# Routing scales as stacked float32r parts, with a reordered head, seam and end, in an attention and gated feed-forward kernel

## The chip, the cores and the metric

The kernel runs on one core of one Trainium2 chip. The metric is the device time of one execution in microseconds (us); lower is better. A profile is one execution taken apart by engine: PE (TensorE, matrix products), DVE (VectorE), ACT (ScalarE), POOL (GpSimd) and SP (SyncE, which here issues most of the transfers).

## The reference

Four sequences of 512 tokens with 1024 channels go through one layer. All is float32.

```python
xn = layernorm(x)                        # over the 1024 channels, no scale or shift
q, k, v = xn @ Wq, xn @ Wk, xn @ Wv      # 16 heads of 64; rotary embedding on q and k
attn = softmax(causal(q @ k.T) / 8)
s = (attn @ v) @ Wo
routing = softmax(xn @ gate_w.T)         # 8 experts
in_scale = routing @ in_channel_scale    # 8 x 1024
out_scale = routing @ out_channel_scale  # 8 x 1024
f = ((xn * in_scale) @ sign(weight).T) * out_scale + bias
out = x + s * silu(f)
```

## The kernel before

Tokens are cut in tiles of 128 (four to a sequence). Activations lie transposed in SBUF, with channels on the partitions. Projections and the output product use one level of Strassen's scheme with seven products (`form_w`, `form_x` and `form_a` build the sums S and T on DVE), in float32. The order of TensorE is written out by hand (`manual_schedule(engines={PE})` at L69), and in the head that of DVE and ACT as well. Elsewhere the Tile scheduler orders the instructions of DVE, ACT, POOL and SP; a call wrapped in `keep_in_program_order` keeps its place.

There are four stages.

*The head* (L612 to L638) loads four token tiles and the first weights. `statistics` (L158) takes two bn halves, their aggregate and a standard deviation on ACT; `normalize` (L172) scales a tile; `transpose_x` (L183) turns it by PE, and ACT copies it to X. The first four matmuls of `project(0, 0)` stand between the transposes of tiles 1 and 2.

*The attention stage* loops over 16 groups (4 sequences by 4 groups of two head pairs; L682). Each step projects the group k (`project`, L263) and weaves in the pieces of group k-1's attention: scores (L370), softmax on DVE, ACT and POOL, transposes of the probabilities (`transpose_p`, L435), values (L449). In the first group of a sequence `router` (L474) computes its routing: 32 small matmuls, softmax, a transpose, and a store of the eight rows per tile to `rt_d` in DRAM. `make_sign` (L524) makes the signs of the feed-forward weight.

*The seam* (L829 to L858) holds the attention of the last group, together with the feed-forward of the first two token pairs. `dense` issues a piece of the feed-forward and `sum_wo` (L764) a piece of the Strassen sums t1 to t4 of Wo.

*The output stage* (L953) loops over eight pairs q of token tiles: `project_out` (L879) is the seven-product output projection. Between its products stand the scales of pair q+1; then follows its feed-forward `ffn` (L773).

The scales are products with only eight contraction rows, one per expert. `load_xn` (L538) places the eight rows of routing at partitions 0, 32, 64 and 96 by four SP transfers; `in_scales` (L563) then runs 16 matmuls of 128 columns over the four row groups and multiplies the activations by the result; `out_scales` (L595) runs four of 512 columns. Both are float32. `split` (L582) cuts the scaled activations into HI, rounded to float32r, and LO, the rest; the ff product with the signs is two float32r matmuls per chunk.

*The end* is the last `project_out`: product 4, product 3, eviction by DVE, stores by POOL (a whole row tile) and SP (two half tiles).

Of the kernel before, what the change touches and what calls it, by code (L numbers as in the profile page):

```python
# [51 lines left out]
def attn_gated_ffn_kernel(  # L52
# [45 lines left out]
    isc = cp.tile([P, E], F32, name="isc")  # L98
    osc = cp.tile([P, E], F32, name="osc")
# [6 lines left out]
    rt_d = dp.tile([B, TPB, NE, P], F32, name="rt_d")  # L106
# [49 lines left out]
    MV = {}  # L156

    def statistics(b, t):  # L158
        xt = xin[b, t]
        stats = st.tile([P, 2, 6], F32, tag="bn", name=f"bn_{b}_{t}")  # L160
        for j in range(2):

            tc.keep_in_program_order(
                nc.vector.bn_stats(stats[:, j, :], xt[:, j * HALF : (j + 1) * HALF])
            )
        mv = st.tile([P, 2], F32, tag="mv", name=f"mv_{b}_{t}")
        nc.vector.bn_aggr(mv, stats)
        std = st.tile([P, 1], F32, tag="std", name=f"std_{b}_{t}")
        nc.scalar.activation(std, mv[:, 1:2], AF.Sqrt, bias=eps)
        MV[b, t] = mv, std  # L170
# [8 lines left out]
    def layernorm(b, t):  # L179
        statistics(b, t)  # L180
        normalize(b, t)

    def transpose_x(b, t, g):  # L183
# [8 lines left out]
        if g == 0 and b > 0:  # L192
            nc.vector.tensor_copy(dst, tp)
        else:
            nc.scalar.copy(dst, tp)
# [67 lines left out]
    def project(b, g):  # L263

        for m in range(3):
# [56 lines left out]
            yield from product(r, SF[key, 3], TF[b, 3])  # L322
            yield from product(p, SF[key, 2], TF[b, 2])
# [7 lines left out]
            ps, p, r = halves(3)  # L331
            yield from product(r, SF[key, 1], TF[b, 1])
# [141 lines left out]
    def router(b, step):  # L474
        if step == 0:
# [10 lines left out]
            R["lg"] = st.tile([P, P], F32, tag="r", name=f"lgs_{b}", bufs=2)  # L486
            nc.scalar.copy(R["lg"], lg)
        elif step == 1:
# [5 lines left out]
            ex = st.tile([P, TPB, 32], F32, tag="r", name=f"rex_{b}", bufs=2)  # L494
            nc.gpsimd.memset(ex, 0.0)
# [11 lines left out]
            )  # L507
            R["ex"] = ex
        else:
            rt = bank(f"rt_{b}")[:, :P]  # L510
            nc.tensor.transpose(rt, R["ex"].rearrange("p t e -> p (t e)"), ident)
            rT = st.tile([P, P], F32, tag="r", name=f"rT_{b}", bufs=2)
            nc.vector.tensor_copy(rT, rt)
            for t in range(TPB):
                nc.sync.dma_start(out=rt_d[b, t], in_=rT[32 * t : 32 * t + NE, :])


    staged = {}

    def load_sign(n):  # L520
        staged[n] = xip.tile([P, E], F32, tag="x", name=f"wb_{n}")
        nc.sync.dma_start(out=staged[n], in_=wb[n // 4, n % 4])

# [14 lines left out]
    def load_xn(q):  # L538
# [10 lines left out]
        RT[q] = rtp.tile([P, 2, P], F32, tag="rt", name=f"rt_{q}")  # L549
        for j in range(4):  # L550
            nc.sync.dma_start(
                out=RT[q][32 * j : 32 * j + NE, :, :],
# [10 lines left out]
    def in_scales(q, banks=ring_banks):  # L563

        ps = [v.rearrange("p (i r q) -> p i r q", i=2, r=2) for v in banks(f"is_{q}")]
        for r in range(2):
            for i in range(2):
                for j in range(4):
                    p0, c = 32 * j, 4 * r + j
                    nc.tensor.matmul(  # L570
                        ps[j][:, i, r, :],
                        lhsT=isc[p0 : p0 + NE, c * P : (c + 1) * P],
                        rhs=RT[q][p0 : p0 + NE, i, :],
                        start=True,
                        stop=True,
                    )
        by_j = XP[q].rearrange("p i (r j) q -> p i r j q", j=4)
        for j in range(4):
            xs = by_j[:, :, :, j, :]
            nc.vector.tensor_tensor(xs, xs, ps[j], op=ALU.mult)  # L580

    def split(q):  # L582

        HI[q] = hl.tile([P, 2, NC, P], F32R, tag="hi", name=f"hi_{q}")
        LO[q] = hl.tile([P, 2, NC, P], F32R, tag="lo", name=f"lo_{q}")
        for i in range(2):
            for c in range(0, NC, 4):
                xs, hi, lo = (v[:, i, c : c + 4, :] for v in (XP[q], HI[q], LO[q]))
                nc.scalar.copy(hi, xs)
                nc.vector.tensor_tensor(lo, xs, hi.bitcast(F32), op=ALU.subtract)  # L590
# [4 lines left out]
    def out_scales(q, banks=ring_banks):  # L595
        ps = banks(f"os_{q}")
        for n in range(4):
# [3 lines left out]
                lhsT=RT[q][32 * n : 32 * n + NE, i, :],  # L601
                rhs=osc[32 * n : 32 * n + NE, k * HALF : (k + 1) * HALF],
# [9 lines left out]
    for t in range(TPB):  # L612
        load_x(0, t)
    for m in range(3):
# [3 lines left out]
    nc.sync.dma_start(out=gw[:, :, :NE], in_=gate_wT.rearrange("(c p) e -> p c e", p=P))  # L618

    first = project(0, 0)  # L620
    with tc.manual_schedule(engines={DVE, ACT}):
        statistics(0, 0)
        for t in range(TPB):
            if t + 1 < TPB:
                statistics(0, t + 1)
            if t == 2:
                next(first)
            normalize(0, t)
            for g in range(2):
                transpose_x(0, t, g)  # L630
            for _ in range((0, 3, 3, 0)[t]):
                next(first)
        for n in (3, 1, 2):
            form_w(keys[0], n)
        next(first)
        for n in (3, 1, 2, 4):
            form_x(0, n)
# [44 lines left out]
    for k, (b, g) in enumerate(groups):  # L682
# [3 lines left out]
        if k == 1:  # L686
            for t in range(TPB):
                nc.sync.dma_start(out=isc[32 * t : 32 * t + NE, :], in_=in_scale)
                nc.sync.dma_start(out=osc[32 * t : 32 * t + NE, :], in_=out_scale)
        extra = []  # L690
        if g == 0:
            extra = [lambda s=s: router(b, s) for s in range(3)]
# [12 lines left out]
        if g == 0:  # L705
            extra += [
                lambda: (load_sign(2 * b), load_sign(2 * b + 1)),
                lambda: None,
                lambda: make_sign(2 * b),
                lambda: make_sign(2 * b + 1),  # L710
            ]

        step = max(1, (len(pieces) + len(extra)) // (len(extra) + 1))
        for n, e in enumerate(extra):
            pieces.insert(min(len(pieces), (n + 1) * step + n), e)
        if b == B - 1:
# [310 lines left out]
```

## Time and profile before

| what | value |
|---|---|
| median of three runs | 1200.04 us (1199.61 to 1200.54) |
| the profiled execution's own time | 1199.76 us |
| its span | 1198.0 us |
| PE busy | 1176.7 us (98%) |
| DVE busy | 751.4 us (63%) |
| POOL busy | 515.8 us (43%) |
| ACT busy | 490.1 us (41%) |

The span runs from the first to the last event of the profile; the time of an execution is a little longer. A line of a view gives start, duration, engine, source line, operation and tiles (output first). What stands in brackets is idle time of the engine just before, and what ended it. The ends of matmuls are modelled, so the distance between starts says how long PE was held. A float32 matmul leaves two records, a float32r matmul one.

### The profile page before, as it was taken

To read this page: it belongs to the slowest core of one execution; us is meant where nothing else is said; L and a number is where in the kernel's file an instruction comes from. 1 tells how busy PE (TensorE), PEld (TensorE's weight loads), DVE (VectorE), ACT (ScalarE), POOL (GpSimd) and SP (SyncE) were. 2 spreads that over 40 slices of the span, in tenths; PEclk is the share of its full clock that TensorE was granted. 3 is DMA by queue.
4 is the path that set the end of the run, shared out by engine and by line. 5 is a ranking of instruction groups with operands and counts; after the bars stand their busy time and mean duration, and the time that the engine had idled before them with its cause. 6 is when DMAs were issued, how large, how long until landed. Compare 5 with 4: busy or idle time off the path is not lost.

```text
span 1198.0 us, 18167 instructions
## 1 busy us (share of the span) xinstructions
PE 1176.7 (98%) x6920; PEld 892.5 (74%) x6920; DVE 751.4 (63%) x1365; ACT 490.1 (41%) x1132; POOL 515.8 (43%) x565
## 2 busy tenths in 40 slices
PE   7999999999999999999999999999999999999998
PEld 5988888887888887788888878788664546655663
DVE  7767777676767767676776766656673543354342
ACT  3464545445465534546553443545431221122120
POOL 0462535245253524435353534525436334533543
PEclk9999999999999999999999999999999999999999
DMA  9423233222233313223234221210505412431320
GB/s 309 143 71 113 91 106 115 80 80 89 86 108 99 128 61 101 80 84 119 82 114 149 80 80 47 86 44 29 195 20 189 162 50 93 141 119 59 106 71 35
DMA packets 57127, 120.28 MB, mean 100 GB/s; under 512 B 4624, under 2 KB 38032, under 8 KB 50896
## 3 DMA queue, kind: packets, MB, share of 16 engines
q1 hardware_dynamic: 54880, 111.26, 28.5%
q0 software_dynamic: 2160, 7.87, 1.6%
q8 instruction: 54, 0.88, 0.3%
q14 instruction: 33, 0.27, 0.1%
HBM read 93.88 MB, written 25.23 MB: 99 GB/s over the span
## 4 chain that ended last, share of the span: by engine, by line
PE 91%; DVE 5%; ACT 2%; issue 1%; POOL 0%; DMA 0%; ACTq 0%; DVEq 0%
PE pj L284 33%; PE wo L891 16%; PE pj L292 13%; PE ff L779 9%; PE ptp L441 6%; PE pv L457 6%; PE sc L375 5%; PE xtp L189 1%; DVE nmx L390 1%; ACT p L393 1%; PE is L570 1%; PE os L599 1%; DVE sg L530 1%; ACT sw L254 1%; ACT sw L253 0%
## 5 line engine op out<-in xcount | busy, mean ns | idle before, releaser
L403 POOL TENSOR_SCALAR p<-p,rs 128x128 f32<-128x128 f32 (+3 forms) x256 | 170.5, 679 | 180.0 <-DVE rs L401 180.0
L393 ACT ACTIVATE p<-sc,nmx 128x128 f32<-128x128 f32 (+3 forms) x256 | 132.4, 523 | 159.7 <-DVE nmx L390 157.0
L284 PE MATMUL pj<-T,S 128*128 128x256 f32 x768 | 183.1, 381 | 0.1
L284 PEld LDWEIGHTS pj<-T,S 128*128 128x128 f32 x768 | 139.8, 190 | 19.2 <-issue 2.3
L339 POOL TENSOR_TENSOR part<-part,part 128x256 f32<-128x256 f32 x48 | 35.2, 734 | 227.4 <-ACT part L338 206.7
L284 PE MATMUL pj<-X,w 128*128 128x256 f32 x512 | 122.9, 381 | 0.0
L256 POOL TENSOR_TENSOR sw<-sw,sin_sb 128x512 f32<-128x512 f32 x64 | 84.1, 1314 | 86.4 <-ACT sw L254 86.4
L233 DVE TENSOR_TENSOR S<-w 128x512 f32<-128x512 f32 x96 | 81.8, 853 | 39.2 <-PE pj L284 34.0
L390 DVE TENSOR_REDUCE nmx<-sc 128x2 f32<-128x512 f32 (+3 forms) x128 | 103.6, 820 | 2.5
L779 PE MATMUL ff<-sg,hi 128*128 128x512 f32 x256 | 103.5, 404 | 0.0
L441 PE MATMUL ptp<-ident,p 128*128 128x128 f32 x640 | 95.6, 273 | 6.9 <-POOL p L403 4.8
L284 PEld LDWEIGHTS pj<-X,w 128*128 128x128 f32 x512 | 92.8, 191 | 11.5 <-issue 0.5
L779 PE MATMUL ff<-sg,lo 128*128 128x512 f32 x256 | 99.8, 390 | 0.0
L447 ACT COPY pT<-ptp 128x512 f32<-128x512 f32 x96 | 56.0, 586 | 99.5 <-PE ptp L441 99.0
L441 PEld LDWEIGHTS ptp<-ident,p 128*128 128x128 f32 x640 | 78.4, 141 | 23.0 <-POOL p L403 6.0
L292 PE MATMUL pj<-S,T 128*128 128x128 f32 x768 | 92.1, 277 | 0.0
L253 ACT ACTIVATE sw<-c 32x512 f32<-32x512 f32 x128 | 80.4, 628 | 22.9 <-DVE c L311 21.1
L292 PEld LDWEIGHTS pj<-S,T 128*128 128x128 f32 x768 | 88.1, 192 | 1.7
L257 POOL TENSOR_TENSOR rot<-rot,sw 128x512 f32<-128x512 f32 x64 | 82.7, 1292 | 4.8
L375 PE MATMUL sc<-rot,rot 64*128 64x384 f32 (+3 forms) x512 | 82.0, 449 | 0.0
L254 ACT ACTIVATE sw<-c 32x512 f32<-32x512 f32 x128 | 80.4, 628 | 1.7
L457 PE MATMUL pv<-pT,v 128*64 128x256 f32 (+3 forms) x512 | 76.0, 439 | 0.0
(123 smaller groups left out, 1961.8 us busy)
## 6 DMA issues: line engine op xcount, KB each, us to landing
w<-in_wqkv SPq DMA_DIRECT2D x48, 1024.0 KB
x<-in_x SPq DMA_DIRECT2D x16, 512.0 KB
xn_d<-X SPq DMA_DIRECT2D x16, 512.0 KB
at_d<-at SPq DMA_DIRECT2D x32, 256.0 KB
xp<-xn_d SPq DMA_DIRECT2D x16, 512.0 KB
ap<-at_d SPq DMA_DIRECT2D x16, 512.0 KB
xr<-in_x SPq DMA_DIRECT2D x16, 512.0 KB
wb<-in_wb SPq DMA_DIRECT2D x8, 512.0 KB
```

What stands on the lines that cost most here:

```text
L254: nc.scalar.activation(sw[r + 32 : r + 64, :], c[r : r + 32, :], AF.Copy, scale=sc)
L256: nc.gpsimd.tensor_tensor(sw, sw, sin_sb, op=ALU.mult)
L284: nc.tensor.matmul(ps, lhsT=wq[:, k, :], rhs=xq[:, k, :], start=(k == 0), stop=(k == 3))
L292: nc.tensor.matmul(ps[:, j * P : (j + 1) * P], lhsT=xq[:, k, j * P : (j + 1) * P], rhs=wq[:, k, :], start=(k == 0), stop=(k == 3),)
L375: nc.tensor.matmul(ps[:, h, :], lhsT=Q[u][r : r + D, i * P : (i + 1) * P], rhs=K[u][r : r + D, : (i + 1) * P], start=True, stop=True,)
L390: nc.vector.tensor_reduce(nmx, ps, AX.X, ALU.max, negate=True)
L393: nc.scalar.activation(pt[:, h, :], ps[:, h, :], AF.Exp, bias=nmx[:, h : h + 1], accum_out=ssum[:, h : h + 1],)
L403: nc.gpsimd.tensor_scalar(pt[:, h, :], pt[:, h, :], rs[:, h : h + 1], 1.0, op0=ALU.mult, op1=ALU.mult,)
L441: nc.tensor.transpose(tp[:, k, :], probs(u, i)[:, h, j * P : (j + 1) * P], ident)
L457: nc.tensor.matmul(pv[r : r + D, j * P :], lhsT=V[u][:, j, r : r + D], rhs=PT[u][:, n, o : o + (TPB - j) * P], start=(j == 0), stop=(j == ...
L779: nc.tensor.matmul(acc, lhsT=part[q][:, i, c, :], rhs=sg[4 * k + c // 2][:, (c % 2) * HALF : (c % 2 + 1) * HALF], start=(c == 0 and part i ...
L891: nc.tensor.matmul(ps, lhsT=lhs[:, k, :], rhs=rhs[:, k, :], start=(k == 0), stop=(k == 3))
```

## The change

*Scales.* Routing and channel scales are each split into a float32r part and the exact rest, and stacked in 32 rows instead of 8: the routing rows are (high, high, low, low), the scale rows alternate between high and low by blocks of eight, so that one float32r product over 32 rows sums all four combinations. `router` makes the routing parts with five more DVE operations; `load_scales` loads each scale table sixteen times over by small SP transfers, and `split_scales` makes its parts on ACT and DVE, selected by the column `is_high`. Scale matmuls become 8 of 256 columns and 4 of 512, all float32r with 32 rows. The routing loads go through POOL's queue.

*Order.* The pieces of the router have fixed places; the first sequence's group 0 holds the scale splitting, and the signs are made in groups 4, 8, 12 and 13 instead of 0, 4, 8 and 12. The very first weight runs product (S1, T1) before (S2, T2).

*Head.* 42 transposes of the identity come first, and 14 more after the first tile. bn halves are interleaved with the normalization; the first weight is loaded by halves between the tiles; the last X copy goes to DVE.

*Seam.* `split` works by token tile i, with two buffers of half the size. `sum_wo` keeps program order, and the t4 sums move here from the first `project_out`.

*End.* For the last pair, what can be combined ahead of a product is combined on POOL (`ahead_of`); product 3 is computed in two halves of 256 columns; stores go by half tiles and quarter tiles over SP and ACT.

The core of the diff:

```diff
+    high = cp.tile([P, 8], F32, name="high")
...
-        if g == 0 and b > 0:
+        if (g == 0 and b > 0) or (g == 1 and (b, t) == (0, TPB - 1)):
             nc.vector.tensor_copy(dst, tp)
...
             yield from product(r, SF[key, 3], TF[b, 3])
+            if pos == 0:
+                bank3 = halves(3)
+                yield from product(bank3[2], SF[key, 1], TF[b, 1])
             yield from product(p, SF[key, 2], TF[b, 2])
...
+            hi = st.tile([P, TPB, NE], F32R, tag="rhi", name=f"rhi_{b}", bufs=1)
+            nc.vector.tensor_copy(hi, exv)
+            hi = hi.bitcast(F32)
+            for n in (3, 2):
+                nc.vector.tensor_tensor(
+                    ex[:, :, n * NE : (n + 1) * NE], exv, hi, op=ALU.subtract
+                )
+            for n in (1, 0):
+                nc.vector.tensor_copy(ex[:, :, n * NE : (n + 1) * NE], hi)
...
+    def load_scales(src):
+        v = xip.tile([P, E], F32, tag="x", name="scales")
+        for t in range(P // NE):
+            nc.sync.dma_start(out=v[NE * t : NE * (t + 1), :], in_=src)
+        scales.append(v)
+
+    def split_scales(dst):
+        v = scales.pop(0)
+        nc.vector.tensor_reduce(is_high[:, 0:1], high, AX.X, ALU.max)
+        nc.vector.tensor_scalar(
+            is_high[:, 1:2], is_high[:, 0:1], -1.0, 1.0, op0=ALU.mult, op1=ALU.add
+        )
+        nc.scalar.copy(dst, v)
+        nc.vector.tensor_tensor(v, v, dst.bitcast(F32), op=ALU.subtract)
+        nc.vector.tensor_scalar(v, v, is_high[:, 1:2], None, op0=ALU.mult)
+        nc.vector.scalar_tensor_tensor(
+            dst, dst.bitcast(F32), is_high[:, 0:1], v, op0=ALU.mult, op1=ALU.add
+        )
...
-        RT[q] = rtp.tile([P, 2, P], F32, tag="rt", name=f"rt_{q}")
+        RT[q] = rtp.tile([P, 2, P], F32R, tag="rt", name=f"rt_{q}")
         for j in range(4):
-            nc.sync.dma_start(
-                out=RT[q][32 * j : 32 * j + NE, :, :],
+            nc.gpsimd.dma_start(
+                out=RT[q][32 * j : 32 * j + 32, :, :],
...
         for r in range(2):
-            for i in range(2):
-                for j in range(4):
-                    p0, c = 32 * j, 4 * r + j
-                    nc.tensor.matmul(
-                        ps[j][:, i, r, :],
-                        lhsT=isc[p0 : p0 + NE, c * P : (c + 1) * P],
-                        rhs=RT[q][p0 : p0 + NE, i, :],
+            for j in range(4):
+                rows, c = slice(32 * j, 32 * j + 32), 4 * r + j
+                nc.tensor.matmul(
+                    ps[j][:, r, :, :],
+                    lhsT=isc[rows, c * P : (c + 1) * P],
+                    rhs=RT[q][rows, :, :],
...
-                lhsT=RT[q][32 * n : 32 * n + NE, i, :],
-                rhs=osc[32 * n : 32 * n + NE, k * HALF : (k + 1) * HALF],
+                lhsT=RT[q][32 * n : 32 * n + 32, i, :],
+                rhs=osc[32 * n : 32 * n + 32, k * HALF : (k + 1) * HALF],
...
+    def keep_warm(n):
+        idle = bank("idle")[:, :P]
+        for _ in range(n):
+            nc.tensor.transpose(idle, ident, ident)
+
+    keep_warm(42)
...
+        half_statistics(0, 0, 0)
+        half_statistics(0, 0, 1)
+        deviation(0, 0)
         for t in range(TPB):
             if t + 1 < TPB:
-                statistics(0, t + 1)
-            if t == 2:
+                half_statistics(0, t + 1, 0)
+            else:
+                form_w(keys[0], 3)
+            normalize(0, t)
+            transpose_x(0, t, 0)
+            if t + 1 < TPB:
+                half_statistics(0, t + 1, 1)
+                deviation(0, t + 1)
+            transpose_x(0, t, 1)
+            if t == 0:
+                keep_warm(14)
+            for _ in range((0, 4, 3, 0)[t]):
                 next(first)
...
-    split(0)
     for n in range(5):
         transpose_p(w, n)
+    split(0, 0)
     scores_1(units)
+    split(0, 1)
     values(w)
...
+    split(1, 0)
     out_scales(1, score_banks)
     dense(gates, 4)
...
-    split(1)
+    split(1, 1)
     scores_02(units)
     gates = gated(1)
-    sums = iter([(2, c) for c in range(4)])
-    dense(gates, 9)
+    dense(gates, 5)
+    sums = iter([(n, c) for n in (2, 4) for c in range(4)])
+    dense(gates, 5)
...
+        def ahead_of(i, k, u):
+            cols = slice(k * HALF, (k + 1) * HALF)
+            c = work.tile([P, HALF], F32, tag="g", name=f"uz_{i}_{k}")
+            nc.gpsimd.tensor_tensor(c, u, Z[q, i][:, cols], op=ALU.mult)
+            nc.gpsimd.tensor_tensor(c, c, XR[i][:, cols], op=ALU.add)
+            return c
+
+        def finish_last(i, cols, ps, c, queue):
+            z = Z[q, i][:, cols]
+            nc.vector.tensor_tensor(z, ps, z, op=ALU.mult)
+            nc.vector.tensor_tensor(z, z, c, op=ALU.add)
+            queue.dma_start(out=out[rows[i], cols], in_=z)
...
+        c01 = ahead_of(0, 1, u2)
+        nc.sync.dma_start(out=out[rows[1], HALF:], in_=Z[q, 1][:, HALF:])
+        finish_last(1, slice(0, HALF), ps, c10, nc.scalar)
+        for n in range(2):
+            ps = ps_wo.tile([P, TH], F32, tag="wo", name=f"wo_{q}_3_{n}")
+            part_n = slice(n * TH, (n + 1) * TH)
+            for k in range(4):
+                nc.tensor.matmul(
+                    ps,
+                    lhsT=SA[q, 4][:, k, :],
+                    rhs=b22[:, k, part_n],
+                    start=(k == 0),
+                    stop=(k == 3),
+                )
+            finish_last(
+                0, slice(HALF + n * TH, HALF + (n + 1) * TH), ps, c01[:, part_n], (nc.scalar, nc.sync)[n]
+            )
```

## The prediction

> **What bounds the kernel now.** I read the page first: engine shares, then the chain that ended last.
>
> ```profile
> PE 1176.7 (98%) x6920; PEld 892.5 (74%) x6920; DVE 751.4 (63%) x1365; ACT 490.1 (41%) x1132; POOL 515.8 (43%) x565
> PE 91%; DVE 5%; ACT 2%; issue 1%; POOL 0%; DMA 0%; ACTq 0%; DVEq 0%
> ```
>
> TensorE is the bound nearly everywhere. A change can win only by giving PE less to do, or where PE stands idle. The table of stages says where it stands idle.
>
> ```profile
> core 0: us, PE busy (x) PEld busy (x) DVE busy (x) ACT busy (x) POOL busy (x), PEclk, DMA share, GB/s
> 0.00:25.00 25.00, 16.07 (x133) 13.59 (x134) 17.67 (x32) 8.78 (x17) 1.50 (x11) 1.00 0.94 327
> 25.00:838.00 813.00, 808.97 (x5399) 675.04 (x5398) 566.38 (x1077) 402.68 (x959) 356.24 (x414) 1.00 0.28 92
> 838.00:897.40 59.40, 56.51 (x321) 40.05 (x320) 44.16 (x77) 25.10 (x64) 24.60 (x28) 1.00 0.29 104
> 897.40:1168.00 270.60, 270.60 (x1016) 153.05 (x1015) 114.87 (x170) 51.72 (x91) 122.27 (x104) 1.00 0.34 111
> 1168.00:1198.00 30.00, 24.55 (x59) 10.72 (x57) 8.30 (x12) 1.80 (x3) 11.20 (x9) 0.99 0.09 35
> ```
>
> Third column less second: 8.9 us idle in the head, 4.0 in all of the attention stage, 2.9 in the seam, none in the output stage, 5.5 at the end. The PE timeline of one scale step shows the work that the change touches.
>
> ```profile
> 925.74 2.74 PE L891 MATMUL wo<-wo,ap 128*128 128x512 f32 x6
> 928.41 1.17 PE L570 MATMUL is<-rt,isc 8*128 8x128 f32 x32
> 929.52 3.70 PE L891 MATMUL wo<-xp,S 128*128 128x512 f32 x8
> 936.58 1.14 PE L599 MATMUL os<-osc,rt 8*128 8x512 f32 x8
> 937.65 0.70 PE L891 MATMUL wo<-xp,S 128*128 128x512 f32 x1
> ```
>
> Ends are modelled, so I use starts: in_scales holds PE from 928.41 to 929.52 (1.11 us), out_scales from 936.58 to 937.65 (1.07). A float32 matmul leaves two records: 16 matmuls are 32 records.
>
> **What the Trainium skill says.** (1) "FP8 and Floating Point Precision", TensorE Precision Notes: true FP32 takes four passes through the array, reduced-precision FP32 reads the value truncated. The trace agrees: a float32 product of 512 columns takes 2 records at 429 ns, 858 ns; a float32r ff matmul of 512 columns starts every 227 ns (3.8 times less). (2) "TensorE: Matmul & The Clock Gate", Part 3 (packing small matmuls): K=32 matmuls in different row groups run side by side, 4 of N=512 measured 3.07 times faster. Here 8 out_scales records take 1.07 us, 134 ns each against 429 alone, 3.2 times. (3) The same page, Parts 1 and 4: the clock doubles after some 3.4 us of activity, and transposes are said not to count. The head shows
>
> ```profile
> 8.37 1.94 PE L189 MATMUL xtp<-ident,x 128*128 128x128 f32 x8 [8.37 <-DVE x L177]
> 10.59 1.97 PE L189 MATMUL xtp<-ident,x 128*128 128x128 f32 x8 [0.28 <-DVE x L177]
> 14.39 1.04 PE L189 MATMUL xtp<-ident,x 128*128 128x128 f32 x8
> ```
>
> Eight transposes take 1.9 us cold, 1.0 warm; warm came by 14.39, when only 2 us of ordinary matmuls had run. So transposes seem to count, against the page; not proved. (4) "DMA: Bandwidth & Descriptors", SWDGE vs HWDGE: a float32r destination counts as a cast, possible only from GpSimd. That explains why the routing loads move from SP to POOL; before.py has no such load.
>
> **The change, part by part.**
>
> *Scales.* in_scales: 8 float32r matmuls of 256 columns instead of 16 float32 of 128; out_scales: 4 float32r of 512 instead of 4 float32. All four row groups stay in use. Column passes fall to a quarter in both. If all shrinks with them: 1.1/4 = 0.28 us each. If instead a fixed part stays: four groups at the ideal share of 227 ns stream 0.23 us, 0.90 in four passes, so about 0.2 of the 1.1 is fixed, and 0.43 remains. I take 0.40. Eight pairs of token tiles: 8 x (1.11 + 1.07 - 0.80) = **11.0 us**, all on the path, as PE has no idle time around them. Ends: 0 (no side by side) to 12.9; a loss is the rival below.
> Beside it: each router gains five DVE operations of about 0.2 us and loses a memset; split_scales has two 128x1024 sets, some 3.5 us each by the T rows (1.2 to 1.3 us); they stand in group 0, where DVE also loses sign making. DVE is 70% busy in that stage and appears in no PE wait there. 32 small scale loads of about 0.3 us (the isc rows on SP) hold SP for 10 us from about 17 us, but the next weight load has to wait until about 27 us anyway. POOL gets 4 routing loads per pair; an output store occupies it 0.57 to 0.64 us, so 2.5 us per pair against 18 of 41 us busy: covered. They stand ahead of POOL's u2 addition, which has product 4 and 3 (6.9 us) to be late in. SP loses those loads. All these: 0, bounds -1 to +2.
>
> *Head.* The instruction order puts 42 dummy transposes first. Start about 1.5 us (identity ready), 4 us cold at 0.24 (16), 26 warm at 0.11: done at about 8.3. The first normalized tile comes at 7.8 instead of 8.2 (one bn half instead of two ahead of it, less two tiny is_high operations). From there I step through: X copy g0 at 9.0 to 9.5, std_1 behind it in ACT's order at 9.8 (**new: std of t+1 queues behind X copy of t**), normalize 1 ends 10.8, normalize 2 at 13.4, its transposes behind 4 matmuls at 13.9, std_3 at 15.4, S3 in the gap, normalize 3 ends 16.4, last copy (now DVE) 18.2, T3 19.4, T2 and S2 23.6. The T, S products of the first key end at about 27.1; before, at 27.58 with one router transpose of 0.1 among them. Faster transposes are mostly eaten by the new ACT order. Gain **0.4 us**; ends +1.5 (warm early) and -3 (never warm: 42 x 0.24 = 10 us).
>
> *Seam.* Waits of PE in 876 to 900:
>
> ```profile
> PE ptp L441 <- DVE z_t L789: 1.1, 1, 1.1
> PE ptp L441 <- POOL p L403: 0.8, 2, 0.6
> ```
>
> The first is DVE doing t4 sums (1.0 to 1.6 us) ahead of the ff evictions; the second is scores_02 evicted behind 3.6 us of split. Pinned sums put t4 later, and splitting by tile moves half of it ahead. A further 0.8 us at 838 to 846 stems from an lo piece ahead of a pT copy; only part of it leaves, as one wait hangs on a POOL addition that stays. What is late next: POOL p, by about 1 us less. I take **1.8** of 2.8; ends 0.5 and 2.8. The sums now run beside the values; t4 is needed only by product 4.
>
> *End.*
>
> ```profile
> 1192.59 0.70 DVE z_t L940
> ...
> 1193.39 0.69 DVE z_t L941
> ```
>
> Then SP stores 256 KB at 1194.11, beside 512 KB from POOL at 1193.3; DMA is busy until about 1196.7. After: two 256-column halves cost PE nothing (8 records at 216 ns, 1.73 us, twice: 3.46 against 3.43). The last DVE pair is 2 x 0.42 instead of 2 x 0.69: 0.5 us. Row 1 and the first half are stored earlier, from SP and ACT queues, so only 128 KB is left: at 400 GB/s (the DMA row there) 0.3 us instead of 1.9. POOL's c01 must be ready by 1191.3 (chain: p5 at 1186.4, three operations of 1.27: 1190.2). Gain **1.6**; ends 0.5 and 2.2.
>
> *Sum.* 11.0 + 0.4 + 1.8 + 1.6 = 14.8. The profiled execution took 1199.76 us (span 1198.0 and 1.76 around it), 0.28 below the median of 1200.04. 1199.76 - 14.8 = **1185.0 us**.
>
> **Rivals.**
> - *Packing without gain (0.10).* The float32r groups run one after the other: 8 x 114 or 4 x 227 ns is 0.91 us plus 0.2, so 1.1 each as now; scales give 0. For: only full-array float32r is in the trace. Against: float32 packs 3.2 times. 1199.76 - 3.8 = **1196.0**.
> - *Head lost (0.10).* The warm transposes stay cold and end at 11.7, 3.3 us after their tile; the 14 more fall into DVE's wait. 1185.0 + 0.4 + 3 = **1188.4**. For: the page's remark. Against: the head rows above.
> - *Slower (0.03).* On PE in the scale steps, stacked float32r groups run singly and in four passes: in_scales 8 x 0.43, out_scales 4 x 0.86, with 0.4 fixed 7.3 us a pair instead of 2.18, +41 in eight, less 3.8: **1237**. It decides from a pair above 2.65 us. Against: the 227 ns rows are single passes.
> - *Nothing of it moves (0.02)*: scale steps stay, and a late POOL or DVE in the attention stage returns 4 us: **1200**.
>
> **How the numbers follow.** The main case has 0.75; its own range is 1181.5 to 1189 by the ends above (scales 0.28 each, warm early, seam whole: -3.5; POOL p, head and end short: +4). The range 1181.5 to 1192 takes in the head rival and half-packed scales, leaving out packing without gain and the slow cases. About 0.2% (2.4 us) is what a measurement here can tell from no change. Faster by more: 0.95; within: 0.02; slower: 0.03.
>
> **What would show it.** in_scales and out_scales start to next start at 0.3 to 0.5 us each (above 1.0: packing failed); PE's 25 to 838 stage shorter by the scale steps in it, its waits on POOL p still about 4 us; xtp at 1.0 us from the first; first T product at about 19.7; PE waits of 876 to 900 below 1 us; span ending some 3.5 us after the last matmul instead of 5.4. A long first-tile wait behind the dummies, or new PE waits on DVE or POOL after 838, would make me wrong.

## The result, and the profile after

| | before | after |
|---|---|---|
| median of four runs each | 1200.17 us (1199.61 to 1200.54) | 1192.38 us (1191.28 to 1192.48) |
| ratio, 95% interval | | 0.9933 (0.9916 to 0.9951) |
| the profiled execution, its span | 1199.76, 1198.0 us | 1192.43, 1190.7 us |

The changed kernel is 7.8 us faster by the medians; 14.8 had been forecast. Line numbers below are those of the changed kernel unless an experiment or the kernel before is named. First the page's engine shares, its row of granted PE clock, and its share of the chain:

```profile
PE 1174.0 (99%) x6760; PEld 895.1 (75%) x6760; DVE 760.6 (64%) x1397; ACT 492.3 (41%) x1133; POOL 536.5 (45%) x597
PEclk9989999999999999999999999999999999999999
PE 94%; DVE 3%; ACT 1%; DMA 1%; issue 0%; POOL 0%; SPq 0%; ACTq 0%; DVEq 0%
```

PE is busy for less time and nearly all of the span, as meant. But there is an 8 in the clock row, in the third slice, some 60 to 90 us after the start. The table of stages says where PE is idle:

```profile
core 0: us, PE busy (x) PEld busy (x) DVE busy (x) ACT busy (x) POOL busy (x), PEclk, DMA share, GB/s
0.00:25.00 25.00, 21.93 (x188) 19.31 (x189) 16.78 (x31) 6.77 (x15) 1.80 (x13) 1.00 0.93 324
25.00:830.00 805.00, 797.86 (x5246) 664.62 (x5245) 566.43 (x1093) 400.71 (x942) 355.46 (x414) 1.00 0.29 94
830.00:900.00 70.00, 67.96 (x421) 51.28 (x420) 51.82 (x91) 28.68 (x81) 35.35 (x43) 1.00 0.29 100
900.00:1160.00 260.00, 260.00 (x837) 146.27 (x836) 116.34 (x171) 53.72 (x93) 129.76 (x118) 1.00 0.36 117
```

Second column less third: the attention stage, 4.0 us idle before, now has 7.1. The waits of PE name it:

```profile
PE pj L304 <- DVE S L253: 6.1, 1, 6.1
PE ptp L468 <- DVE pT L472: 1.6, 1, 1.6
...
PE ptp L468 <- POOL p L430: 1.0, 2, 0.5
```

A single wait of 6.1 us is new. The waits on POOL p, 4.0 us before, fell to 1.0. The PE timeline of the scale step shows the part that came as forecast:

```profile
929.91 0.51 PE L624 MATMUL is<-rt,isc 32*128 32x256 f32 x8
930.35 3.70 PE L994 MATMUL wo<-xp,S 128*128 128x512 f32 x8
...
937.42 0.50 PE L652 MATMUL os<-osc,rt 32*128 32x512 f32 x4
937.85 3.70 PE L994 MATMUL wo<-xp,S 128*128 128x512 f32 x8
```

From start to next start: in_scales 0.44 us (1.11 before), out_scales 0.43 (1.07). Over eight pairs that is 8 x (2.18 - 0.87) = 10.5 us.

Now the stall. The PE timeline of group 1 before, and the same stretch after:

```profile
55.17 3.72 PE L284 MATMUL pj<-X,w 128*128 128x256 f32 x16
58.73 2.75 PE L284 MATMUL pj<-T,S 128*128 128x256 f32 x12
61.41 1.99 PE L375 MATMUL sc<-rot,rot 64*128 64x512 f32 x8
```

```profile
55.48 3.72 PE L304 MATMUL pj<-X,w 128*128 128x256 f32 x16
65.34 5.04 PE L304 MATMUL pj<-T,S 128*128 128x256 f32 x12 [6.14 <-DVE S L253]
70.31 1.99 PE L402 MATMUL sc<-rot,rot 64*128 64x512 f32 x8
```

The ACT and DVE timeline after, of the same time:

```profile
60.08 1.04 ACT L572 CAST osc<-scales 128x1024 fp32r<-128x1024 f32 x1
61.15 1.33 DVE L573 TENSOR_TENSOR scales<-scales,osc 128x1024 f32<-128x1024 f32 x1 [0.77 <-ACT osc L572]
62.52 0.75 DVE L574 TENSOR_SCALAR scales<-scales,is_high 128x1024 f32<-128x1024 f32 x1
63.31 1.28 DVE L575 SCALAR_TENSOR_TENSOR osc<-osc,is_high,scales 128x1024 fp32r<-128x1024 f32 x1
64.51 1.29 DVE L253 TENSOR_TENSOR S<-w 128x512 f32<-128x512 f32 x2
```

Read from the bottom: PE waits for S3, one of the sums that `form_w` builds, of group 1's first weight. S3 takes 0.69 us and needs nothing new: PE had used the raw weight without a wait at 55.48. But in DVE's in-order queue it stands behind the three operations that split the out scales (61.15 to 64.51, 3.4 us; the texts on record say 3.3), and these wait for their cast on ACT, which stands behind the first softmax's exponentials in ACT's queue. After the gap the 12 records hold PE from 65.34 to 70.31, 0.41 us each against 0.22 for the same records of before (58.73 to 61.41): another 2.3 us lost to the clock, which the view grants at 0.55 there. From start to start the gap itself costs 6.3 us (55.48 to 65.34, before 55.17 to 58.73), so 8.6 us together; the texts on record below split the same sum as 6.1 and 2.5.

### The profile page after: what moved, and what is told of

Its sections match the earlier page's. It is cut to its first block, busy times and chain, and to the rows that moved or that the text cites. A ratio compares the mean times of both kernels' runs of the same rounds, so it can differ in the third digit from the quotient of the medians.

```text
span 1190.7 us, 17943 instructions
## 1 busy us (share of the span) xinstructions
PE 1174.0 (99%) x6760; PEld 895.1 (75%) x6760; DVE 760.6 (64%) x1397; ACT 492.3 (41%) x1133; POOL 536.5 (45%) x597
## 4 chain that ended last, share of the span: by engine, by line
PE 94%; DVE 3%; ACT 1%; DMA 1%; issue 0%; POOL 0%; SPq 0%; ACTq 0%; DVEq 0%
PE pj L304 33%; PE wo L994 16%; PE pj L312 16%; PE ff L874 9%; PE sc L402 6%; PE pv L484 6%; PE ptp L468 6%; PE xtp L209 1%; DVE nmx L417 1%; ACT p L420 1%; PE lg L506 1%; DMA x<-in_x 1%; DVE sc L413 0%; PE os L652 0%; PE is L624 0%
## 5 line engine op out<-in xcount | busy, mean ns | idle before, releaser
L430 POOL TENSOR_SCALAR p<-p,rs 128x128 f32<-128x128 f32 (+3 forms) x256 | 167.9, 669 | 182.5 <-DVE rs L428 182.5
L276 POOL TENSOR_TENSOR sw<-sw,sin_sb 128x512 f32<-128x512 f32 x64 | 85.6, 1337 | 90.2 <-ACT sw L274 90.2
L253 DVE TENSOR_TENSOR S<-w 128x512 f32<-128x512 f32 x96 | 78.4, 818 | 30.8 <-PE pj L304 27.0
L277 POOL TENSOR_TENSOR rot<-rot,sw 128x512 f32<-128x512 f32 x64 | 83.0, 1297 | 4.9
```

The lines of the kernel that those rows point to most:

```text
L276: nc.gpsimd.tensor_tensor(sw, sw, sin_sb, op=ALU.mult)
L277: nc.gpsimd.tensor_tensor(rot, rot, sw, op=ALU.add)
L430: nc.gpsimd.tensor_scalar(pt[:, h, :], pt[:, h, :], rs[:, h : h + 1], 1.0, op0=ALU.mult, op1=ALU.mult,)
```

## The experiments

Two theories of the stall stood against each other at first: the *place* of the split operations in DVE's queue, and the *32 small loads* of the scale tables, which held SP's queue (0.29 us each, all but one of them between 20.6 and 33.6 us) and so delayed the next weight. Two rows cut each run into comparable parts, whatever moved ahead of them: the start of the products (X, S) of the first key (27.58 us before, 27.78 after) ends the head, and "the v row", the transposes that wait for DVE v at the seam's beginning (840.52 and 844.18), ends the attention stage.

### e1: one transfer per scale table

```diff
-        for t in range(P // NE):
-            nc.sync.dma_start(out=v[NE * t : NE * (t + 1), :], in_=src)
+        nc.sync.dma_start(out=v, in_=src[None, :, :].to_broadcast((P // NE, NE, E)))
```

> The changed kernel, but each scale table is loaded by one SP transfer that repeats its eight rows, in place of sixteen. Theory A: the 6.1 us stall of PE at 59 us comes from DVE's order in group 1 (S3 of group 1's first weight, L253, stands behind the osc split), and that order was made because the 32 small loads hold SP's queue ahead of that weight's load. With one load the weight goes out at about 28 us instead of 33.7, S3 stands ahead of the first softmax, the stall is gone and the time is 1192.4 - 6.1 = 1186.3. Rival B: PE at that place is short of something else (the new splitting work on DVE and ACT itself is too much for group 0): the stall stays above 3 us and the time above 1189.

1190.71 us (ratio to before 0.9921, 0.9906 to 0.9936). The wait on S went, and another came in the router:

```profile
41.88 0.45 PE L547 MATMUL rt<-ident,rex 128*128 128x128 f32 x1 [4.65 <-DVE is_high L567]
```

With the tables there early, three of the splits' operations came between the small operations of the router's softmax on DVE (30.4 to 41.7 us). The clock fell again: 0.89 over 30 to 60 us. So the loads only decided *where* in DVE's queue the splits fell; taking them away moved the stall.

A second cost rides on this one. The router's last small operations, pushed back, ran beside the rotary products on POOL (L276 and L277, from 35.25 us on). The DVE timeline of e1, then that of the changed kernel, where these operations were done by 33.5, before POOL's products began at 34.08:

```profile
36.00 1.29 DVE L531 TENSOR_TENSOR rex<-rex,rrs 128x32 f32<-128x32 f32 x1
37.55 1.07 DVE L536 CAST rhi<-rex 128x32 fp32r<-128x32 f32 x1
```

```profile
32.46 0.19 DVE L531 TENSOR_TENSOR rex<-rex,rrs 128x32 f32<-128x32 f32 x1
32.69 0.18 DVE L536 CAST rhi<-rex 128x32 fp32r<-128x32 f32 x1
```

L531 to L543 took 4.8 us in e1 and 1.0 us in the changed kernel. How much of the 4.65 us is this and how much the splits themselves was not tried apart.

### e2: the three DVE operations of the out split left out

```diff
         nc.scalar.copy(dst, v)
+        if dst is osc:
+            return
         nc.vector.tensor_tensor(v, v, dst.bitcast(F32), op=ALU.subtract)
```

The low parts of the out scales are missing from its result.

> The changed kernel with its 32 loads; the three DVE operations of the osc split (L573 to L575) are left out, so that the low parts of the out scales are missing. Theory A: S3 of group 1 then starts right after the last softmax reciprocal, at about 60.5 instead of 64.5, and PE waits about 2 us instead of 6.1; time about 1188.3. Rival (the late weight load itself holds S3): S3 stays at 64 us or later, PE still waits about 6 us, time about 1192.

1185.55 us in the one run, PEclk full in every slice. All 32 loads were kept, and this is what stayed of the wait (PE timeline):

```profile
60.66 2.83 PE L304 MATMUL pj<-T,S 128*128 128x256 f32 x12 [1.92 <-DVE S L253]
```

4.2 us less wait and 6.9 us less time: most of the difference is the clock, which a gap of 1.9 us left at full speed (12 records in 2.76 us instead of 4.97). The three operations ahead of S3 were the cause of 4.2 us of the wait; the other 1.9 us stayed with the loads.

### e3: the stacked scales alone

The kernel before, with float32r scales and one transfer per table; head, the router's pieces, the seam's order and the end as before. Its HI and LO buffers are already the half-size ones, and the signs stand in groups 4, 8, 12 and 13.

> The kernel before with the stacked float32r scales alone (one load per table; router places, head, seam and end as before; the signs in groups 4, 8, 12 and 13). If the scale steps are worth what their starts show (8 x (2.18 - 0.87) = 10.5 us) and nothing comes back elsewhere: 1200.2 - 10.5 = 1189.7. If the five router operations and the splits cost time in the attention stage: above 1191.

1193.42 us (0.9949, 0.9932 to 0.9966): 6.4 us gained, not 10.5, though the half-size buffers, a gain of their own (e14 to e16 below), are in it. Its waits of PE:

```profile
PE rt L550 <- DVE rex L546: 3.0, 1, 3.0
PE ptp L471 <- POOL p L433: 2.9, 3, 1.4
```

The scales alone already bring the router's stall, and here too the router's last operations (L534 to L546 of e3) ran beside POOL and took 4.5 us.

### e4: the pieces of router and signs in groups 4, 8 and 12 as before

The kernel of e1 with the old places of these pieces.

> As e1, but in groups 4, 8 and 12 the router steps and the sign steps stand where the kernel before had them. Theory: the change took 3.0 us out of PE's waits for POOL p in the attention stage (4.0 to 1.0) by those places alone, so these waits return to about 4 us and the time is about 3 us above e1. Rival: POOL got rid of them by something else (no memset, other DVE order): waits stay at about 1 us, time equal to e1 within 1 us.

1192.68 us in the one run; PE's waits on POOL p are 2.7 us instead of 1.0. From (X, S) to the v row it took 817.4 us, against 815.4 in e1. So the new places of router and sign pieces took out 1.7 of the 3.0 us of waits on POOL p, a gain that the forecast didn't have. The waits did not return to the 4 us expected here; what took out the rest is not shown.

### e5: splits later in group 0, two of their operations on POOL

One transfer per table as in e1, the router's pieces ahead of loads and splits in group 0's list, and:

```diff
...
-        nc.vector.tensor_tensor(v, v, dst.bitcast(F32), op=ALU.subtract)
-        nc.vector.tensor_scalar(v, v, is_high[:, 1:2], None, op0=ALU.mult)
+        nc.gpsimd.tensor_tensor(v, v, dst.bitcast(F32), op=ALU.subtract)
+        nc.gpsimd.tensor_scalar(v, v, is_high[:, 1:2], 1.0, op0=ALU.mult, op1=ALU.mult)
```

> The changed kernel with one transfer per scale table, the router's pieces ahead of the scale loads and splits in group 0, and the two middle operations of each split on POOL instead of DVE. Nothing is left out. Theory A (both gaps, the 6.1 us ahead of the products of S3 in group 1 and the 4.6 us ahead of the router's transpose, come only from the places of the split operations in DVE's in-order queue): no PE wait over 2 us between 25 and 90 us, PEclk full in every slice, time 1192.43 - 6.1 (wait) - 2.5 (records at the half clock after it) = 1183.8 us, within 1 us. Theory B (group 1 would have to wait anyway, for its weight or the exps on ACT): a wait of 4 us or more stays or comes at another tile, and the time is 1188 to 1191 us.

1189.15 us (0.9910, 0.9895 to 0.9924). The wait on S is gone, but theory A missed by 5 us: the router waits again, now as in this DVE timeline.

```profile
25.69 2.29 DVE L253 TENSOR_TENSOR S<-w 128x512 f32<-128x512 f32 x1
...
29.76 2.66 DVE L253 TENSOR_TENSOR S<-S,w 128x512 f32<-128x512 f32 x1
```

These take 0.69 us elsewhere. POOL's subtractions ran from 25.08 to 27.43 and from 29.52 to 31.87. The Trainium skill, "SBUF — State Buffer", Terms, says that DVE and POOL share a port pair, held for a whole instruction, and that the loser blocks; the two rows, which end 0.55 us after POOL's, agree. The router's transpose then waited 3.2 us (and 0.7 for its logits), and the clock was 0.95 over 35 us, 1.75 us: 1183.8 + 3.9 + 1.75 = 1189.45, near the 1189.15 measured. Moving work from DVE to POOL did not take it off DVE's time.

### e6, e7, e8: the head

> The kernel of e5 with the head as before the change: whole weight loads after the x tiles, statistics in one piece, no dummy transposes, first weight in the old order of products. Nothing is left out. Theory A (the new head is worth what the forecast gave it): 0.4 us slower than e5, up to 3 us if the dummies matter more. Theory B (the new head gains nothing, as its third x tile now stands behind half a weight in the queue; the first pj_4 stood at 27.78 against 27.58 before): 0.2 us faster than e5, that is the same within what is measured.

> The kernel of e5 with the third x tile's load ahead of the first half of the first weight. Nothing is left out. Theory A (the late third tile, 1.1 us of DVE waiting on its transfer, is what ate the head's gain): DVE's wait on in_x goes, the transposes of tiles 2 and 3 and the first T, S products come 0.5 to 1.1 us earlier, time 0.5 to 1.1 us less than e5. Theory B (the head is bound by the half weight or by DVE's own chain): the wait moves to S3 or to another tile, first T, S product at the same time within 0.2 us, time the same.

> The kernel of e5 without the 42 and the 14 dummy transposes, all else of the new head kept. Nothing that the result needs is left out. Theory A (transposes alone warm the clock, and it matters): the first 8 transposes take 1.9 us instead of 1.1, the next 8 too, and the products of the first key come 0.8 to 1.7 us later. Theory B (transposes don't count[...]; something else warms the clock): the first 8 transposes take 1.1 us here too. Theory C (they warm it, but PE waits for DVE's normalized tiles anyway): the first 8 take 1.9 us, and the first T, S product comes less than 0.5 us later than in e5.

e6 took 1191.01 us, e7 1188.93, e8 1190.99 (one run). The totals can't be compared: in e6 the POOL operations fell on the rotary products (4.6 us of PE waits on POOL rot). The start of the (X, S) products says more: 27.97 in e5, 27.79 with the old head (e6), 28.00 with the third tile first (e7), 29.66 without the dummies (e8). But it scatters: over all traces it lies between 27.11 and 28.10 with the new head (eleven kernels, mean 27.6) and between 27.46 and 28.21 with the old one (five, mean 27.8). A gain of 0.4 us can be neither seen nor excluded in this. A of e7 did not come (its dummies ended at 8.42 instead of 7.94, its first (T, S) product came at 20.09 instead of 19.75). The dummies are worth 1.7 us, clear of the scatter, *in the new order*; the old order has none and starts (X, S) no later. The PE timeline of e8 shows what they do:

```profile
7.91 1.94 PE L209 MATMUL xtp<-ident,x 128*128 128x128 f32 x8 [7.91 <-DVE x L195]
10.94 1.97 PE L209 MATMUL xtp<-ident,x 128*128 128x128 f32 x8 [1.08 <-DVE x L195]
12.73 3.78 PE L304 MATMUL pj<-X,w 128*128 128x256 f32 x8
```

### e9: the splits in group 4

One transfer per table, and the loads and splits taken out of group 0:

```diff
...
+        if k == 4:
+            pieces.insert(8, lambda: split_scales(osc))
+            pieces.insert(4, lambda: split_scales(isc))
+            pieces.insert(0, lambda: (load_scales(in_scale), load_scales(out_scale)))
-        if k in (4, 8, 12, 13):
-            n = {4: 0, 8: 2, 12: 4, 13: 6}[k]
+        if k in (8, 12, 13, 14):
+            n = {8: 0, 12: 2, 13: 4, 14: 6}[k]
```

> The changed kernel with one transfer per scale table, and the scale loads and both splits moved out of group 0 into group 4; the signs go from groups 4, 8, 12, 13 to 8, 12, 13, 14. The split's operations stay on DVE. Nothing is left out. Theory A (the lost time is the place of the split operations in DVE's queue while the router and the first softmax are due): no PE wait over 1 us from 25 to 90 us, PEclk full in every slice, and 1192.43 - 6.1 (wait) - 2.5 (half clock) = 1183.8 us, within 1 us. Theory B (3.3 us of DVE work per split always make PE late, wherever they stand): a PE wait of 3 us or more on DVE in group 4, 270 to 320 us, and 1187 us or more.

1187.20 us (0.9891, 0.9874 to 0.9907). No wait of PE between 28 and 202 us, and yet 3.4 us of the loss stayed (3.8 in the profiled execution, 1187.56). PE timeline, then the table of that stretch:

```profile
204.38 3.47 PE L304 MATMUL pj<-X,w 128*128 128x256 f32 x8 [2.04 <-issue]
```

```profile
202.00:212.00 10.00, 7.96 (x35) 6.57 (x35) 9.86 (x18) 4.55 (x16) 6.09 (x9) 0.83 0.56 200
```

The scheduler puts the out split at 192.7 to 197.1 us, within group 3; DVE is busy 9.86 of the ten microseconds from 202 us on, and the eviction of a product bank (L331, until 204.27) comes late; the gap ends 0.1 us after it, though the view names no releaser. That the split is what made it late was argued here and is tried in e13. A gap of 2.0 us, then eight records at the half clock (3.26 us instead of 1.73) and four slow transposes (0.66 instead of 0.44): 3.8 us. (The text on record of e13 counts 16 records and 1.6 us.)

### e10, e11, e12: head, seam and end on this base

> The kernel of e9 with the head as before the change (whole weight loads behind the x tiles, statistics in one piece, no dummy transposes, the first weight's products in the old order). Nothing is left out. Theory A (the new head gains the 0.4 us of the forecast): 0.4 us slower than e9. Theory B (the new head gains nothing; its products of S1 of the first key started at 27.8 to 28.0 us in the runs so far, against 27.6 to 27.8 with the old one): the same to 0.2 us faster than e9, and that product at 27.6 to 27.8.

> The kernel of e9 with the seam as before the change (split by half of the channels in one piece for both tiles, Wo's sums not pinned, t4 sums in the first output projection). Nothing is left out. Forecast (1.8 us from the seam): 1.8 us slower than e9. Rival (the waits only changed place: a wait of 1.6 us on DVE's copy of pT came for those that went): 0.7 us slower, the difference in PE idle between 830 and 900 us.

> The kernel of e9 with the end as before the change (last product 3 in one piece, eviction and stores as before). Nothing is left out. Forecast (1.6 us from the end): 1.6 us slower than e9. Rival (half of the gain is lost to DVE additions of 0.97 to 1.20 us beside POOL, and to the last small store): 1.0 us slower, the span ending 5.4 us after the last matmul instead of 4.4.

*Head* (e10): 1186.91 us, and (X, S) at 27.46 against 27.57 in e9. The same, within the scatter.

*Seam* (e11): 1187.08 us. Its gap at 204 us was 1.88 us and left the clock full, so the part behind it has to be compared: from the v row to the last product 3, 338.28 us in e11 and 338.48 in e9. The seam's new order is worth nothing. (The text on record calls the old split one piece; e11 issues it as two calls in a row and keeps the half-size buffers.)

*End* (e12): 1189.64 us, 2.4 slower. From the start of the last product 3 to the end of the span 10.06 us, against 7.99 in e9.

### e13: a shorter split

e9 with two DVE operations fewer of table size in each split:

```diff
...
+        nc.vector.tensor_scalar(
+            is_high[:, 0:1], is_high[:, 0:1], 2.0, -1.0, op0=ALU.mult, op1=ALU.add
+        )
         nc.scalar.copy(dst, v)
-        nc.vector.tensor_tensor(v, v, dst.bitcast(F32), op=ALU.subtract)
-        nc.vector.tensor_scalar(v, v, is_high[:, 1:2], None, op0=ALU.mult)
+        nc.gpsimd.tensor_scalar(v, v, is_high[:, 1:2], 1.0, op0=ALU.mult, op1=ALU.mult)
```

> The kernel of e9 with a shorter split: the low rows' selection on POOL straight from the table, then one DVE operation hi * (high - low) + v * low, so that each split holds DVE's queue for 1.3 us instead of 3.3. Nothing is left out. Theory A (in e9 the osc split, 192.7 to 197.1 us, pushed DVE's evictions behind the first products of group 4, whose gap of 2.0 us and 16 records at the half clock, 1.6 us, are the 3.4 us above 1183.8): no gap at 202 us, PEclk full there, time 1183.6 us, within 0.8. Theory B (the gap at 202 us comes from the transfers of the scale tables, which delay a weight or an x tile in SP's queue): the gap stays at 2 us and the time at 1187 us.

1185.72 us (0.9883, 0.9868 to 0.9898), clock full everywhere:

```profile
202.00:212.00 10.00, 9.71 (x59) 8.58 (x58) 9.89 (x18) 4.35 (x14) 5.53 (x8) 1.00 0.64 213
```

The transfers stayed and the gap went: theory A, though 1.3 us past its bound. The rest can be placed by the scores of group 3 that start at 182.43 us here and at 190.70 in the changed kernel: from (X, S) that is 154.33 against 162.92 us, so the first stall had cost **8.6 us**, the sum of gap and clock read above. From there to the next scores of that kind it is 35.86 us here and 34.21 there, 1.65 lost to small waits around what is left of the split.

### e14, e15, e16: what the seam is worth

> The kernel of e13 with the seam as before the change. Nothing is left out. Theory A (the new seam costs PE 0.8 us: 2.03 us idle between 830 and 900 us in e9 against 1.26 in e11, as its pinned sums hold DVE's copy of pT): 0.8 us faster than e13. Theory B (the forecast: the new seam saves PE 1.8 us): 1.8 us slower.

> The kernel before the change with one edit: HI and LO lie in two buffers of half the size, one for each token tile, instead of one buffer for both. Nothing is left out. Theory A (what gains in the seam is this buffering: the split of the next pair can start when the first tile's products are done, and no longer stands ahead of the last scores' eviction): PE's waits between 876 and 900 us fall from 1.9 to about 0.4 us, and the stretch from the transpose behind v at 840.5 us to the last product 3 shrinks by 1.5 us. Theory B (the seam's waits went because of the shorter scales): waits and stretch as before, 1.9 and 348.4 us.

> The kernel of e14 with HI and LO in one buffer for both tiles, as before the change; so all of the seam is as before. Nothing is left out. Theory A (the buffering is the seam's gain): waits of about 1.9 us between 872 and 900 us, and 1.5 us slower than e14, a stretch of 340.0 us against 338.5. Theory B (the scales took the seam's waits out): as e14, 338.5 us.

| kernel | HI, LO buffers | order in the seam | v row to last product 3 | median |
|---|---|---|---|---|
| before | whole | old | 348.44 us | 1200.17 us |
| e15 | half | old | 345.86 us | 1197.11 us |
| e13 | half | new | 338.43 us | 1185.72 us |
| e14 | half | old | 338.48 us | 1185.44 us |
| e16 | whole | old | 340.02 us | 1186.87 us |

e14 is the same as e13: no sign of A's 0.8, nor of B's 1.8. e15, the kernel before with the buffers alone, is faster: 0.9977 (0.9968 to 0.9986). Its stretch is 2.6 us shorter than before's, where A had 1.5; why the buffers are worth more beside the old scales is not shown. e16 lies where A put it, 340.0. In its PE timeline the old waits are back, row by row:

```profile
875.53 0.66 PE L468 MATMUL ptp<-ident,p 128*128 128x128 f32 x4 [0.56 <-POOL p L430]
876.41 0.66 PE L468 MATMUL ptp<-ident,p 128*128 128x128 f32 x4 [0.22 <-POOL p L430]
879.14 1.43 PE L468 MATMUL ptp<-ident,p 128*128 128x128 f32 x8 [1.14 <-DVE z_t L888]
```

So the seam's gain is the buffering, 1.5 us between e14 and e16. The new order adds a wait of its own, 1.6 us in the waits list shown first: in the DVE timeline of the changed kernel a pinned sum stands ahead of the copy of pT that PE needs. It takes 1.76 us instead of 0.69, beside a POOL addition (L885, 884.66 to 886.37).

```profile
885.15 1.76 DVE L865 TENSOR_TENSOR z_t<-wo,xp 128x512 f32<-128x512 f32 x1
886.84 1.28 DVE L472 COPY pT<-ptp 128x512 f32<-128x512 f32 x2
```

e13 and e14, at 0.9883 of the time before (0.9868 to 0.9898 and 0.9866 to 0.9899), are the fastest kernels here that leave nothing out; the changed kernel is at 0.9933.

## Why the prediction was right or wrong

The direction was right; the time, 1185.0 us forecast, was 7.4 us too low. Term by term, from the traces of before and after (the seam's is 348.44 - 338.48 between v row and last product 3, less the 8.5 us of the 6 in_scales and 7 out_scales in between; "beside it" is the 8.6 us above):

| term | forecast | measured |
|---|---|---|
| scales on PE | -11.0 | -10.5 |
| head, to (X, S) | -0.4 | +0.2 (27.58 to 27.78), within a scatter of 1 us |
| waits on POOL p in the attention stage | 0 | -3.0 |
| seam | -1.8 | -1.5 |
| end, from the last product 3 | -1.6 | -1.0 (9.04 to 8.04) |
| work "beside it" | 0 | +8.6 |
| sum | -14.8 | -7.2 (spans: 1198.0 to 1190.7) |

**The step that failed** is "All these: 0, bounds -1 to +2". The forecast priced the split well (3.5 us a set) and hid it behind "DVE is 70% busy in that stage and appears in no PE wait there". That is an average. What counts is who stands behind the operation in DVE's in-order queue at that moment: S3 of the next weight, with PE behind it. And the split didn't only take 3.4 us: it also waited for its cast on ACT, with S3 behind it all the while. The forecast had the 32 loads over by the time the next weight can go out, about 27 us; they held SP to 33.6 us, and that weight went out at 33.71 instead of 27.78. It was still in time, but the forecast did not ask when the loaded tables let the *splits* start, nor whom they then met. e2 shows the operations ahead of S3 as the cause, e1 that without the loads they strike elsewhere, and e13 that the 8.6 us go when the splits leave group 0 and are short. The price of the clock after a gap, 2.3 of the 8.6 us, was in no bound either.

**Scales.** Right in mechanism and nearly in size: 0.87 us a pair against the 0.80 taken. The split into a fixed 0.2 and a streaming part gave 0.43 each, and that was the measured value; the lower number had been picked for no reason that the profile gave.

**Head.** The mechanism assumed (fast transposes from the first, eaten by the new order of ACT) is half right: they run at 1.09 us for eight, and no gain is seen above the scatter. The forecast had (X, S) at 27.1 and the first T product at 19.7; they came at 27.78 and 20.56. One loss had not been seen: the third x tile's transfer stands behind half a weight, DVE waits 1.1 us for it in the middle of the second tile's work, and that tile's transposes come at 11.50. With the same head DVE waits only 0.36 us for it in e5, so part of the scatter lies there. In e7, with that tile first, no gain is seen either.

**Attention stage.** The waits on POOL p were to stay "about 4 us"; they fell to 1.0. e4 ties 1.7 of these 3.0 us to the places of router and sign pieces. Which operation of theirs had stood ahead of POOL was not tried.

**Seam.** The size was nearly right and the reason wrong: not the pinned sums, not the place of the second half, but the two half-size buffers, which the forecast had not priced at all. Its own sign, waits below 1 us, did not come: one of 1.6 us stands at 887.57, from the pinned sums that were to help.

**End.** From the start of the last product 3 to the end of the span the new end takes about 8.0 us in every trace (7.98 to 8.09). The old one took 9.04 or 9.05 in two (before, e15) and 10.06 in two (e3, e12), so its gain is 1.0 or 2.0 us; the 1.6 forecast lies between. The two lengths of the old end are not in the kernel's work: the last store is issued 5.15 us after that start in all four, and the traffic of the stores ends about 7.5 us after it. With the new end that traffic ends about 5.8 us after it, 1.7 us earlier, near the 1.6 forecast. What differs is the time from there to the end of the span: about 1.5 us (before, e15), 2.6 us (e3, e12) and, with the new end, 2.2 us. No view shows work in it; why it differs stays open. A loss of the new end's own is seen in DVE's additions beside POOL: 1.20 us for 512 columns (0.69 elsewhere) and 0.97 us for 256, where the last one takes 0.42.

**Rivals.** "Packing without gain" had its number near the result by chance (1196.0); its mechanism is refuted by the scale rows. "Head lost" is refuted too: the dummies warmed the clock. "Nothing of it moves" named a late DVE in the attention stage, 4 us, but gave it 0.02 and tied it to scale steps that stay. What was missing was what happened: the scales gain, and a one-time operation in a full queue takes most of it back. In the range, the three lower ends of the main case add up to 4.0 us (1.9, 1.1 and 1.0), not 3.5; nothing hangs on it.

## What to carry to other kernels

Work that runs once is not free because its engine is 70% busy: look up what stands behind it in the in-order queue, what it waits for itself, and which instruction of the bounding engine needs that. Here a transfer that landed earlier (e1) and operations moved to another engine (e5) changed the place of the collision. Moving the splits to group 4 (e9) brought 5.2 us, and making them shorter there (e13) another 1.5 us; a shorter split in group 0 was not tried. And price a gap of the tensor engine by its length and by the clock that may follow it.

## What the hardware showed beyond that

*Transposes warm the clock.* The Trainium skill, "TensorE: Matmul & The Clock Gate", Part 4, says that they don't count as activity. In the changed kernel only 42 transposes of the identity preceded the first tile's, and those eight took 1.09 us; without dummies (e8) they took 1.94. Here they count.

*The length of a gap does not alone decide the clock after it.* The same page (Part 1, HAM oscillation) gives idle gaps above about 3.4 us as the danger. After 4.65 us (e1) and 6.14 us (after) the next records did run at half speed, but so they did after 2.04 us (e9, PEclk 0.56 over those eight). Gaps of 1.88 (e11), 1.92 (e2), 2.03 (e10) and 2.12 us (e12) left the clock full, as this PE line of e10 shows beside e9's of 3.47 us:

```profile
204.26 1.97 PE L307 MATMUL pj<-X,w 128*128 128x256 f32 x8 [2.03 <-issue]
```

So a gap of about 2 us can bring the half clock, and a slightly longer one can leave it full; what else decides was not measured.
